# Moving two inlets of a state space layer beside its first scans, and their convolution from VectorE to TensorE

## The chip, the cores and the metric

The kernel runs on one core of a Trainium2 chip. TensorE (PE in the profile) multiplies matrices into PSUM, which the kernel uses as eight tiles filled in turn; VectorE (DVE) and ScalarE (ACT) read PSUM and work on SBUF; GpSimd (POOL) works on SBUF; SyncE (SP) and the sequencers of ACT and POOL issue DMA transfers. The metric is the device time of one execution in microseconds (us), the median over several executions.

## The reference

Two layers of a Perceiver-like block over 16 sequences of 64 tokens (1024 tokens of width 256). Layer 0 has a cross attention over 1601 context rows, a causal self attention and a feed forward part chosen by position; layer 1 has a second cross attention, a state space layer and a mixture of 64 experts. Every part adds to the residual x. The change lies in the state space layer:

```python
proj = x @ W_in.T                       # x is the layer norm of the residual
x_inner, z = proj[..., :d], proj[..., d:2 * d]          # d = 512
xc = conv(x_inner, conv_w, padding=[(3, 0)], feature_group_count=d) + conv_b
x_conv = silu(xc)                       # four taps per channel, each channel alone
dt = softplus(dt_proj + dt_bias); dA = exp(A * dt); dB = B_proj * dt
h = dA_t * h + dB_t * x_t               # scan over 64 tokens of each sequence
y_t = C_t @ h
y = (y + D * x_heads) * silu(z);  out = y @ W_out.T
```

## The kernel before, in words

The 1024 tokens are eight groups (NG = 8) of 128, two sequences in each. A group of the state space layer goes through three generators.

`inlet(g, ...)` (from L276) makes the layer norm of a group, transposes it (`psx_ss`, L285), projects it to `x_inner` (`ps_xi`, L291: eight products of 128x128x128, each of which the profile counts as two MATMULs) and to dt (`ps_dt`, L296), and copies `x_inner` to `xp`, a tile with three zeros ahead of each sequence's 64 tokens (L293). The convolution then runs channel by partition: ACT makes the first tap with the bias (L300, four instructions of 128x128) and DVE adds the other three (L304, twelve instructions of 128x128). Weights and bias are halved beforehand (`cwh`, `cbh`), so that silu is (tanh(v)+1)*v (L309, L310). Four transposes (`ps_xt`, L314) and a copy put the result in `xtok`, where the scans read it.

`sums(lo, hi)` waits for the inlets of four groups, turns their dt into softplus by a chain of small DVE instructions (L330 to L351), multiplies by a constant matrix (`ps_seg`, L356) and writes the sums to a DRAM buffer `segd` (L358, ACT's queue).

`scan(g)` computes a group's scan as matrix products over six halving levels. It loads `e` from `segd`, spread over partitions (L1336, SP's queue, two transfers of 896 KB a group), takes exponentials on ACT (L1343), projects B and C (L1350, L1357), forms `bt` (L1352), the scaled copies `pb` and `pc` (L1367 on DVE, L1369 half on POOL and half on DVE) and `pd` (L1377, POOL, reads `cT` and `bt`), projects z (L1382), forms the 128x128 matrices `gt` level by level (`ps_g`, L1400; L1408, L1417), multiplies `xtok` by them (`ps_y`, L1433), and adds the output product to x (`ps_o`, L1446, L1447). `route(g)` then picks the experts of the group and queues its rows for `post`, which scatters them with indirect DMAs on POOL (L1163).

The order in which PE gets this work is written by a planner, `drive`. Each generator yields (cost, gap): the planner advances its own clock by the cost, and calls the generator again no sooner than the gap after. Among the generators whose time has come it takes the first kind listed. The listed number is how many of one kind are open at once; a scan that has yielded "tail" no longer counts. The tile framework places instructions on each engine's queue near this order, fills the buffers of a tag in turn, and adds the waits.

There are two drives around the change. The first (L1109) holds all of layer 0 and the second cross attention, and in its list stand six inlets (g = 0 to 5, two at once) and `sums(0, 4)`. Then the pools of the first phase close, and `w2` and `wrk3` take over their memory: a tile of the second phase waits for what lay there before. The second drive (L1481) holds the inlets 6 and 7, `sums(4, 8)`, eight scans (two at once), and `outward` and `shared`. The tiles `bt`, `cT2` and `yT` of a scan have two buffers each, as `wrk3` gives by default.

Of the kernel before, what the change touches and what calls it, by code (L numbers as in the profile page):

```python
# [10 lines left out]
F32 = mybir.dt.float32  # L11
I32 = mybir.dt.int32
U32 = mybir.dt.uint32
AF = mybir.ActivationFunctionType
ALU = mybir.AluOpType
# [3 lines left out]
P = 128  # L19
B, S, D = 16, 64, 256  # L20
NTOK = B * S
NG = NTOK // P
# [8 lines left out]
DI = 512  # L31
# [110 lines left out]
def _bc(ap, axis, n):  # L142

    v = ap.unsqueeze(axis)
    shape = list(v.shape)
    shape[axis] = n
    return v.to_broadcast(shape)
# [3 lines left out]
def perceiver_kernel(ctx: ExitStack, tc: tile.TileContext, a: dict, consts: bass.AP, out: bass.AP):  # L151
    nc = tc.nc
    V, A, G, T = nc.vector, nc.scalar, nc.gpsimd, nc.tensor
# [7 lines left out]
    def const(name, rows=P):  # L161
        at, width = _COLS[name]
        return ct[:rows, at : at + width]
# [5 lines left out]
    ident = const("ident")  # L169
# [8 lines left out]
    ones = cst.tile([1, P], F32, name="ones")  # L178
# [12 lines left out]
    def evac(dst, src):  # L191

        flip[0] ^= 1
        if flip[0]:
            V.tensor_copy(dst, src)
        else:
            A.copy(dst, src)  # L197

    def layernorm(src, name, xn, parted=False, beside=None, behind=None):

        st = small.tile([P, 6], F32, tag="ln_st", name=f"st_{name}")
        V.bn_stats(st, src)
        mv = small.tile([P, 2], F32, tag="ln_mv", name=f"mv_{name}")
        V.bn_aggr(mv, st)
        ve = small.tile([P, 1], F32, tag="ln_ve", name=f"ve_{name}")
        V.tensor_scalar(ve, mv[:, 1:2], 1e-5, None, ALU.add)  # L206
        rs = small.tile([P, 1], F32, tag="ln_rs", name=f"rs_{name}")
        root = G.tensor_tensor(rs, ve, neghalf[:, 0:1], ALU.pow)  # L208
        if behind is not None:
            after(root, [behind])  # L210
        if beside is None:
            yield 0, 1.8
        else:
            for _ in range(3):
                yield next(beside)
        if parted:

            src, to = src.rearrange("p (k c) -> p k c", c=2), xn.rearrange("p (c k) -> p k c", c=2)
        else:
            to = xn  # L220
        V.tensor_scalar(to, src, mv[:, 0:1], rs, ALU.subtract, ALU.mult)
        if beside is not None:
            yield from beside
# [6 lines left out]
    pst = psm = psb  # L230
# [38 lines left out]
    sw = {"done": 0, "routed": 0, "half": 0, "made": 0}  # L269
    segd = dram.tile([NG * NH, (NL + 1) * P], F32, name="segd")  # L270

    def until(test):
        while not test():
            yield 0, 0.5

    def inlet(g, tile1, tile2):  # L276
        yield from until(lambda: "winT" in sw)
        xnT, winT = sw["xnT"], sw["winT"]
        tk = slice(g * P, (g + 1) * P)
        xn = tile1([P, D], f"xn_ss{g}")  # L280
        yield from layernorm(x[:, g, :], f"ss{g}", xn)
        yield 0, 0.9
        pt = pst([P, 2, P], f"psx_ss{g}")
        for c in range(2):
            T.transpose(pt[:, c, :], xn[:, c * P : (c + 1) * P], ident)  # L285
        evac(xnT[:, :, tk], pt)
        yield 0.3, 0.6
        pm = psm([P, 4, P], f"ps_xi_{g}")
        for j in range(4):
            for c in range(2):  # L290
                T.matmul(pm[:, j, :], lhsT=winT[:, c, j, :], rhs=xnT[:, c, tk], start=c == 0, stop=c == 1)  # L291
        xp = sw["xps"][g % 2]
        A.copy(xp[:, :, :, 3 : S + 3], pm.rearrange("p j (b t) -> p j b t", b=2))  # L293
        pm = psm([P, NH], f"ps_dt_{g}")
        for c in range(2):
            T.matmul(pm, lhsT=xnT[:, c, tk], rhs=sw["wdtT"][:, c, :], start=c == 0, stop=c == 1)  # L296
        V.tensor_tensor(sw["dtr"][:, g, :], pm, sw["dtb"], ALU.add)
        xc = tile2([P, 4, 2, S], f"xc_{g}")
        for j in range(4):
            A.activation(xc[:, j, :, :], xp[:, j, :, 0:S], AF.Identity, bias=sw["cbh"][:, j : j + 1], scale=sw["cwh"][:, j, 0:1])  # L300
        yield 2.2, 0.6
        for j in range(4):
            for k in range(1, 4):
                V.scalar_tensor_tensor(xc[:, j, :, :], xp[:, j, :, k : k + S], sw["cwh"][:, j, k : k + 1], xc[:, j, :, :], ALU.mult, ALU.add)  # L304
            if j < 3:
                yield 0, 0.8
        xcf = xc.rearrange("p j b t -> p (j b t)")
        th = tile2([P, 512], f"xth_{g}")
        A.activation(th, xcf, AF.Tanh)  # L309
        V.scalar_tensor_tensor(xcf, th, 1.0, xcf, ALU.add, ALU.mult)  # L310
        yield 0, 2.2
        pt = pst([P, 4, P], f"ps_xt_{g}")
        for j in range(4):
            T.transpose(pt[:, j, :], xcf[:, j * P : (j + 1) * P], ident)  # L314
        evac(sw["xtok"][:, g, :], pt.rearrange("p j k -> p (j k)"))
        sw["done"] += 1
        yield 0.55, 0
# [46 lines left out]
    with ExitStack() as p1:  # L364
        w1 = p1.enter_context(tc.tile_pool(name="w1", bufs=1))
        wrk = p1.enter_context(tc.tile_pool(name="wk", bufs=2))
# [7 lines left out]
        def tile1(shape, name):  # L374

            return wrk.tile(shape, F32, tag="k", bufs=15, name=name)

        def tile2(shape, name):

            return wrk.tile(shape, F32, tag="d", bufs=9, name=name)  # L380
# [46 lines left out]
        for name in ("L0_attn_q_norm_w", "L0_attn_k_norm_w"):  # L427
            src = a[name]
            nc.scalar.dma_start(
                out=rows[at[0] : at[0] + 1, :].rearrange("r (h d) -> r h d", d=HD),  # L430
                in_=_bc(src.unsqueeze(0), 1, 8),
# [86 lines left out]
        pm = psm([P, D], "ps_m0")  # L518
# [587 lines left out]
        def maker(gen, *args):  # L1106
            return lambda: gen(*args)

        drive(  # L1109
            (2, [maker(chain, 0), prepare] + [maker(chain, g) for g in range(1, NG)]),  # L1110
            (1, [prepare_ssm]),
            (2, [maker(inlet, g, tile1, tile2) for g in range(NG - 2)]),
            (1, [maker(sums, 0, 4)]),
        )

# [17 lines left out]
    xtok, xnTm = sw["xtok"], sw["xnT"]  # L1133
# [149 lines left out]
    with p2:  # L1283
        w2 = p2.enter_context(tc.tile_pool(name="w2", bufs=1, reuse_waits="tile"))
        wrk = p2.enter_context(tc.tile_pool(name="wrk3", bufs=2, reuse_waits="tile"))
# [14 lines left out]
        A.activation(Ac, col("L1_attn_A_log", 0, 4), AF.Exp)  # L1300
        V.tensor_scalar(Ac, Ac, BIG, -1.0, ALU.min, ALU.mult)


        pbs = [w2.tile([P, NL, 4, P], F32, name=f"pb{i}") for i in range(2)]
        gts = [w2.tile([P, NH, P], F32, name=f"gt{i}") for i in range(2)]
# [22 lines left out]
        def scan(g):  # L1328
# [6 lines left out]
            for q in range(2):  # L1335
                nc.sync.dma_start(  # L1336
                    out=e[q * 64 : (q + 1) * 64, :, :, :].rearrange("p j l k -> p j (l k)"),
                    in_=src[g, q].partition_broadcast(64),
# [8 lines left out]
            pm = psm([P, 4, P], f"ps_B_{g}")  # L1347
            for j in range(4):
                for c in range(2):
                    T.matmul(pm[:, j, :], lhsT=winT[:, c, 8 + j, :], rhs=xnTm[:, c, tk], start=c == 0, stop=c == 1)  # L1350
            bt = wrk.tile([P, 4, P], F32, tag="bt", name=f"bt_{g}")
            V.tensor_tensor(bt, pm, dts, ALU.mult)  # L1352
            yield 1.8, 0
            pm = psm([P, 4, P], f"ps_C_{g}")
# [4 lines left out]
            cTm = wrk.tile([P, 4, 2, P], F32, tag="cTm", bufs=1, name=f"cTm_{g}")  # L1359
            for q in range(2):  # L1360
                A.activation(cTm[:, :, q, :], pm, AF.Copy, scale=const("nsel")[:, q : q + 1])
            cT = wrk.tile([P, 4, P], F32, tag="cT2", name=f"cT_{g}")
            A.copy(cT, pm)
            pcs = []
            for l in range(NL):
# [14 lines left out]
            pm = psm([P, DI], f"ps_z_{g}")  # L1380
            for c in range(2):
                T.matmul(  # L1382
                    pm,
                    lhsT=xnTm[:, c, tk],
                    rhs=winT[:, c, 4:8, :].rearrange("p j k -> p (j k)"),
                    start=c == 0,
                    stop=c == 1,
# [7 lines left out]
            for l in range(0, NL, 2):  # L1395
                for i in range(2):
                    h = 1 << (l + i)
                    pg = psm([P, NH, 64], f"ps_g_{g}_{l + i}")
                    for j in range(4):
                        T.matmul(  # L1400
                            pg[:, 2 * j : 2 * j + 2, :].rearrange("p q t -> p (q t)"),
                            lhsT=pb[:, l + i, j, :],
                            rhs=pcs[l + i][:, j, :, :].rearrange("p q t -> p (q t)"),
                            start=True,
                            stop=True,
# [16 lines left out]
            pm = psm([P, NH], f"ps_dg_{g}")  # L1422
# [8 lines left out]
            pm = psm([P, NH, 64], f"ps_y_{g}")  # L1431
# [5 lines left out]
            pt = pst([P, 4, P], f"ps_yT_{g}")  # L1437
            for j in range(4):
                T.transpose(pt[:, j, :], yt[:, j * P : (j + 1) * P], ident)
            yT = wrk.tile([P, 4, P], F32, tag="yT", name=f"yT_{g}")  # L1440
            A.copy(yT, pt)
            yield 0.55, 0.7
            yield from until(lambda: "outward" in sw)
            pm = psm([P, D], f"ps_o_{g}")
# [30 lines left out]
        def wide(tag):  # L1475
            return lambda shape, name: wrk.tile(shape, F32, tag=tag, name=name)

        def wtile2(shape, name):
            return wide("xth" if name.startswith("xth") else "xc")(shape, name)

        drive(  # L1481
            (2, [maker(inlet, g, wide("xn"), wtile2) for g in range(NG - 2, NG)]),
            (1, [maker(sums, 4, NG)]),
            (2, [maker(scan, g) for g in range(NG)]),
            (1, [outward, shared]),
        )
# [153 lines left out]
    with tc.If(n > CAP):  # L1640
        with tc.For_i(0, E) as e:
# [9 lines left out]
            for q in range(4):  # L1651
# [12 lines left out]
                for i in range(2):  # L1664
                    g = 2 * q + i
# [36 lines left out]
```

## Time and profile before

| | |
|---|---|
| median of 7 runs | 1077.04 us (1071.03 to 1080.79) |
| profiled execution | 1066.66 us, its span 1064.9 us |
| busy share of the span | PE 80%, DVE 59%, ACT 28%, POOL 26% |
| last product of `fpy` before the first inlet | ends at 542.1 us |
| second cross attention of the last group | ends at 574.4 us |
| transposes of inlet 4, of inlets 6 and 7 | start at 588.0 and 607.4 us |
| first `e` load issued, first exponential of `e` | 606.25 and 621.66 us |
| `bt` of the eight scans | 621.4, 637.3, 670.3, 684.8, 715.0, 734.7, 765.4, 785.7 us |
| last scan adds to x | 825.2 us |
| first row of the experts gathered | 860.05 us |

A line of a group of instructions reads: line, engine, operation, output tile and input tiles, shapes, count, then the busy time in us and the mean of one in ns, then the idle time of that engine just ahead of them and what ended it. The busy time of overlapping matmuls is less than the count times the mean: sixteen MATMULs of 128 columns whose mean is 310 ns take 1.95 us together. A line of the timeline reads: start in us, duration in us, engine, line, operation and tiles, with the idle time ahead in brackets. A line of the table of stretches reads: start and end, length, then the busy time of PE, of weight loads, DVE, ACT and POOL with the number of instructions, the granted clock of TensorE as a share of full speed, the mean busy share of the DMA engines, and GB/s.

### The profile page before, as it was taken

Reading aid. Unit: us, or ns where it says so; the run is one execution under the profiler, and the core shown is the slowest. Engines: PE = TensorE matmul, PEld = TensorE weight load, DVE = VectorE, ACT = ScalarE, POOL = GpSimd, SP = SyncE. Lnnn points to the kernel's source line nnn. Section 1 sums busy time; section 2 is a strip of 40 time slices with the busy share of each in tenths; the row PEclk is TensorE's granted clock in tenths of the full one; section 3 lists DMA queues with packets and bytes.
Section 4 is the critical chain, followed back from the end, with each engine's and each line's share of the span. In section 5 each row is a group of like instructions: output and inputs, shape, how many; then the busy total and the mean of one; then the engine's idle time right before and its main releaser. Section 6 shows DMA issues by size and latency. Waiting matters only on the chain. (4 is left out here: it accounts for less than half of the span.)

```text
span 1064.9 us, 15921 instructions
## 1 busy us (share of the span) xinstructions
PE 853.1 (80%) x5858; PEld 647.5 (61%) x5858; DVE 624.7 (59%) x1863; ACT 294.8 (28%) x672; POOL 273.4 (26%) x302
## 2 busy tenths in 40 slices
PE   4978788988899788988786677978777359999956
PEld 3666555655656555555554565877666248888834
DVE  1446564466646565465566686888887863334316
ACT  0214132332332232241323353433411013323310
POOL 0000100001000101001011122455666525565650
PEclk8889999999999999999979678999887569999988
DMA  7502131310503113101501264344402958998236
GB/s 243 178 27 76 64 134 54 124 46 19 187 1 125 64 59 130 62 1 64 158 3 35 63 142 102 70 122 106 130 24 69 358 189 279 300 304 294 93 123 279
DMA packets 70725, 130.56 MB, mean 123 GB/s; under 512 B 10099, under 2 KB 56623, under 8 KB 67574
## 3 DMA queue, kind: packets, MB, share of 16 engines
q1 hardware_dynamic: 56016, 107.97, 31.3%
q0 software_dynamic: 7680, 17.33, 4.7%
q10 hardware_dynamic: 6950, 4.23, 1.4%
q8 instruction: 47, 0.77, 0.3%
q14 instruction: 32, 0.26, 0.1%
HBM read 97.54 MB, written 36.14 MB: 126 GB/s over the span
## 5 line engine op out<-in xcount | busy, mean ns | idle before, releaser
L1547 POOL DMA_INDIRECT ybuf<-yo,goal x96 | 93.5, 974 | 78.6 <-ACT yo L1573 34.2
L1539 PE MATMUL ps_ee<-xT,wq 128*128 128x192 f32 x512 | 95.4, 330 | 0.0
L1539 PEld LDWEIGHTS ps_ee<-xT,wq 128*128 128x128 f32 x512 | 81.8, 190 | 6.5 <-issue 5.8
L1163 POOL DMA_INDIRECT xbuf<-xtok,idx x64 | 69.8, 1091 | 44.2 <-issue 15.9
L994 PE MATMUL fpy<-fw,fxm 128*128 128x256 f32 x256 | 59.0, 390 | 13.3 <-DVE fxm L991 6.8
L1400 PE MATMUL ps_g<-pc,pb 128*128 128x128 f32 x384 | 56.8, 312 | 15.3 <-POOL pc L1369 7.6
L1400 PEld LDWEIGHTS ps_g<-pc,pb 128*128 128x128 f32 x384 | 55.0, 227 | 18.4 <-POOL pc L1369 16.4
L630 PE MATMUL po_a<-cn,paT_a 128*64 128x256 f32 (+1 forms) x416 | 52.8, 387 | 15.7 <-ACT paT_a L624 7.7
L994 PEld LDWEIGHTS fpy<-fw,fxm 128*128 128x128 f32 x256 | 49.3, 195 | 23.8 <-issue 15.9
L630 PE MATMUL po_b<-cn,paT_b 128*64 128x256 f32 (+1 forms) x416 | 50.2, 385 | 9.2 <-DVE paT_b L624 8.3
L208 POOL TENSOR_TENSOR rs_ff<-ve_ff,neghalf 128x1 f32<-128x1 f32 x8 | 4.4, 548 | 204.7 <-DVE ve_ff L206 193.2
L404 PE MATMUL psc<-ct,cn 128*128 128x128 f32 x384 | 50.4, 282 | 3.2 <-DVE cc_a L570 1.9
L592 PE MATMUL sc_b<-cT,qT_b 128*64 128x512 f32 (+1 forms) x256 | 47.3, 524 | 2.1 <-DVE qT_b L564 1.6
L404 PEld LDWEIGHTS psc<-ct,cn 128*128 128x128 f32 x384 | 45.3, 146 | 5.9 <-issue 3.2
L197 ACT COPY cT<-psc 128x512 f32<-128x512 f32 x51 | 29.8, 589 | 64.4 <-PE psc L404 63.9
L1541 ACT ACTIVATE hg<-ps_ee 128x192 f32<-128x192 f32 x64 | 21.2, 331 | 93.3 <-PE ps_ee L1539 93.3
L1527 PE MATMUL ps_xT<-ct,xg 128*128 128x128 f32 x192 | 30.8, 289 | 20.1 <-DMA xg<-xbuf 20.1
L592 PE MATMUL sc_a<-cT,qT_a 128*64 128x512 f32 (+1 forms) x256 | 46.4, 505 | 0.0
L630 PEld LDWEIGHTS po_a<-cn,paT_a 128*64 128x64 f32 (+1 forms) x416 | 26.8, 136 | 31.7 <-ACT paT_a L624 8.7
L630 PEld LDWEIGHTS po_b<-cn,paT_b 128*64 128x64 f32 (+1 forms) x416 | 27.7, 136 | 25.4 <-DVE paT_b L624 10.0
L208 POOL TENSOR_TENSOR rs_ml<-ve_ml,neghalf 128x1 f32<-128x1 f32 x8 | 5.6, 703 | 142.0 <-DVE ve_ml L206 142.0
L1527 PEld LDWEIGHTS ps_xT<-ct,xg 128*128 128x128 f32 x192 | 24.2, 148 | 28.5 <-DMA xg<-xbuf 20.3
(443 smaller groups left out, 1877.4 us busy)
## 6 DMA issues: line engine op xcount, KB each, us to landing
cn<-in_ctx_dram SPq DMA_DIRECT2D x16, 1536.0 KB
e<-segd SPq DMA_DIRECT2D x16, 896.0 KB
xbuf<-zero SPq DMA_DIRECT2D x8, 1632.0 KB
xg<-xbuf SPq DMA_DIRECT2D x16, 816.0 KB
wq<-in_L_ffn_We_gate_dram SPq DMA_DIRECT2D x16, 512.0 KB
wq<-in_L_ffn_We_up_dram SPq DMA_DIRECT2D x16, 512.0 KB
wq<-in_L_ffn_We_down_dram SPq DMA_DIRECT2D x16, 512.0 KB
yg<-ybuf SPq DMA_DIRECT2D x8, 1024.0 KB
```

The costliest lines, as they stand in the source:

```text
L197: A.copy(dst, src)
L208: root = G.tensor_tensor(rs, ve, neghalf[:, 0:1], ALU.pow)
L404: T.transpose(ps[:, j, :], cn[:, 4 * q + j, c * P : (c + 1) * P], ident)
L592: T.matmul(sc[b * 64 : (b + 1) * 64, :], lhsT=qT[:, c, b * 64 : (b + 1) * 64], rhs=cTs[2 * g + b][:, c, 512 * j : 512 * j + n], start=c == ...
L630: T.matmul(pos[j > 0][b * 64 : (b + 1) * 64, :], lhsT=paTs[j][:, i, b * 64 : (b + 1) * 64], rhs=cns[2 * g + b][0:r, k, :], start=k in (0, ...
L994: T.matmul(py, lhsT=xm[:, t, c, :], rhs=fw[:, 2 * h + t, c, :], start=h + t + c == 0, stop=h == 3 and t == 1 and c == 1,)
L1163: sct = G.indirect_dma_start(out=xbuf, out_offset=bass.IndirectOffsetOnAxis(ap=idx[:, g, k : k + 1], axis=0), in_=xtok[:, g, 0:DX], in_off ...
L1400: T.matmul(pg[:, 2 * j : 2 * j + 2, :].rearrange("p q t -> p (q t)"), lhsT=pb[:, l + i, j, :], rhs=pcs[l + i][:, j, :, :].rearrange("p q t ...
L1527: T.transpose(to, xgs[q][:, 2 * part + s, c * P : (c + 1) * P], ident)
L1539: T.matmul(pe[:, j, :], lhsT=w, rhs=xTs[q][:, i, c, :], start=c == 0, stop=c == 1)
L1541: A.activation(hg, pe[:, 0, :], AF.Silu)
L1547: arr = G.indirect_dma_start(out=ybuf, out_offset=bass.IndirectOffsetOnAxis(ap=goal, axis=0), in_=y, in_offset=None, bounds_check=NTOK * T ...
```

## The change

Inlets 4 and 5 leave the first drive and stand with 6 and 7 in the second, again two at once, beside the scans. In the second phase an inlet finds `taps`, sixteen diagonal 128x128 matrices (four channel blocks, four taps) made there by DVE, and `cbr`, the halved bias as a row, which comes by a DMA on ACT's queue and a multiplication on POOL. Its convolution is then sixteen products of a diagonal with a shifted view of `xp`, and four products of the bias row with a row of ones, all accumulated in one PSUM tile `ps_cv`; tanh and the last product read that tile, and ACT alone copies the transposed result. Inlets 0 to 3 keep their convolution on ACT and DVE. `bt`, `cT2` and `yT` get one buffer each.

```diff
@@ inlet
         V.tensor_tensor(sw["dtr"][:, g, :], pm, sw["dtb"], ALU.add)
+        if "taps" in sw:
+            yield 2.2, 1.0
+            pm = psm([P, 4, P], f"ps_cv_{g}")
+            for j in range(4):
+                for k in range(4):
+                    T.matmul(pm[:, j, :].rearrange("p (b t) -> p b t", b=2), lhsT=sw["taps"][:, j, k, :], rhs=xp[:, j, :, k : k + S], start=k == 0, stop=False)
+                T.matmul(pm[:, j, :], lhsT=sw["cbr"][:, j * P : (j + 1) * P], rhs=ones, start=False, stop=True)
+            th = tile2([P, 512], f"xth_{g}")
+            pmf = pm.rearrange("p j k -> p (j k)")
+            A.activation(th, pmf, AF.Tanh)
+            xcf = tile2([P, 512], f"xc_{g}")
+            V.scalar_tensor_tensor(xcf, th, 1.0, pmf, ALU.add, ALU.mult)
+            yield 4.2, 2.0
+            pt = pst([P, 4, P], f"ps_xt_{g}")
+            for j in range(4):
+                T.transpose(pt[:, j, :], xcf[:, j * P : (j + 1) * P], ident)
+            A.copy(sw["xtok"][:, g, :], pt.rearrange("p j k -> p (j k)"))
+            sw["done"] += 1
+            yield 0.55, 0
+            return
         xc = tile2([P, 4, 2, S], f"xc_{g}")
@@ first drive
-            (2, [maker(inlet, g, tile1, tile2) for g in range(NG - 2)]),
+            (2, [maker(inlet, g, tile1, tile2) for g in range(NG // 2)]),
@@ second phase
+        taps = sw["taps"] = w2.tile([P, 4, 4, P], F32, name="taps")
+        for j in range(4):
+            V.tensor_tensor(taps[:, j, :, :], _bc(ident, 1, 4), _bc(sw["cwh"][:, j, :], 2, P), ALU.mult)
+        cbr = sw["cbr"] = w2.tile([1, DI], F32, name="cbr")
+        nc.scalar.dma_start(out=cbr, in_=a["L1_attn_conv_b"].unsqueeze(0))
+        G.tensor_scalar(cbr, cbr, 0.5, None, ALU.mult)
@@ scan: bufs=1 for three tags
-            bt = wrk.tile([P, 4, P], F32, tag="bt", name=f"bt_{g}")
+            bt = wrk.tile([P, 4, P], F32, tag="bt", bufs=1, name=f"bt_{g}")
-            cT = wrk.tile([P, 4, P], F32, tag="cT2", name=f"cT_{g}")
+            cT = wrk.tile([P, 4, P], F32, tag="cT2", bufs=1, name=f"cT_{g}")
-            yT = wrk.tile([P, 4, P], F32, tag="yT", name=f"yT_{g}")
+            yT = wrk.tile([P, 4, P], F32, tag="yT", bufs=1, name=f"yT_{g}")
@@ second drive
-            (2, [maker(inlet, g, wide("xn"), wtile2) for g in range(NG - 2, NG)]),
+            (2, [maker(inlet, g, wide("xn"), wtile2) for g in range(NG // 2, NG)]),
```

## The prediction

> **What bounds the kernel now.** I read the page's slices first: the middle of the span is where PE drops below 8 tenths and its granted clock sinks.
>
> ```profile
> PE   4978788988899788988786677978777359999956
> DVE  1446564466646565465566686888887863334316
> PEclk8889999999999999999979678999887569999988
> ```
>
> The seam between inlets and scans is slices 22 to 25 (559 to 665 us; a slice is 26.6). To see what it consists of I cut it into stretches, from the transposes of inlet 4 (587.8) to the end of scan 2's B product (670.3), the point to which I compare, and the next two pairs of scans.
>
> ```profile
> 587.80:597.70 9.90, 7.05 (x47) 6.35 (x47) 7.52 (x27) 4.76 (x11) 4.51 (x3) 0.81 0.01 2
> 597.70:608.50 10.80, 5.86 (x16) 2.50 (x16) 7.72 (x25) 3.35 (x8) 0.00 (x0) 0.53 0.30 80
> 608.50:620.20 11.70, 11.66 (x77) 10.35 (x76) 7.00 (x28) 6.12 (x14) 0.00 (x0) 0.85 0.98 210
> 620.20:626.90 6.70, 0.03 (x1) 0.06 (x1) 5.42 (x9) 5.00 (x9) 3.01 (x3) 0.65 0.75 152
> 626.90:643.70 16.80, 15.78 (x92) 14.34 (x92) 16.23 (x37) 6.52 (x12) 4.37 (x4) 0.73 0.48 110
> 643.70:649.60 5.90, 0.02 (x1) 0.05 (x2) 5.70 (x8) 0.87 (x3) 4.10 (x3) 0.71 0.00 0
> 649.60:670.30 20.70, 19.81 (x140) 16.55 (x141) 10.07 (x20) 9.57 (x17) 2.63 (x3) 0.92 0.42 96
> 670.30:715.00 44.70, 36.48 (x259) 32.92 (x257) 40.00 (x129) 18.27 (x37) 23.66 (x21) 0.96 0.44 108
> 715.00:765.40 50.40, 39.97 (x275) 36.16 (x273) 42.64 (x131) 14.98 (x33) 30.92 (x29) 0.90 0.47 118
> ```
>
> In the first seven, 82.5 us, PE is busy 60.2 and idle 22.3; where it idles DVE is nearly full, and the clock is 0.53 to 0.85. PE's own waits there:
>
> ```profile
> PE ps_seg L356 <- DVE sp_dt L351: 7.8, 2, 5.9
> PE ps_g L1400 <- DVE pb L1367: 6.7, 1, 6.7
> PE ps_xt L314 <- DVE xc L310: 3.7, 2, 1.9
> PE psx_ss L285 <- DVE xn_ss L221: 1.2, 1, 1.2
> ```
>
> So the seam is paced by DVE (convolutions, softplus chain, pb and pc), and the first `e` load stands behind inlet 5's convolution, as SP's waits say:
>
> ```profile
> SPq L1336 <- DVE xc L310: 27.5, 1, 27.5
> SPq L1336 <- PE ps_xt L314: 1.2, 1, 1.2
> ```
>
> **The prices.**
>
> ```profile
> 573.75 1.95 PE L291 MATMUL ps_xi<-xnTm,winT 128*128 128x128 f32 x16
> 649.58 3.17 PE L356 MATMUL ps_seg<-kmat,sp_dt 128*32 128x512 f32 x4 [5.94 <-DVE sp_dt L351]
> L304 DVE SCALAR_TENSOR_TENSOR xc<-xp,cwh,xc 128x128 f32<-128x128 f32 x96 | 27.5, 351 | 0.8 <-ACT xc L300 0.6
> L1590 DVE TENSOR_TENSOR dgl<-ct,w 128x512 f32<-128x512 f32 x8 | 5.5, 689 | 0.2
> ```
>
> *Convolution on PE.* At full clock 16 MATMULs take 1.95 us, 0.122 each. One inlet has 16 diagonal products and 4 bias products, two MATMULs each: 40 x 0.122 = 4.9 us. Four inlets: 19.5 us added to PE. The bias products have one row of weights; the nearest row with few rows (`ps_ohb`, 8 rows, at a poor clock) is 3.6 us for 16, 0.225 each, so the 32 bias MATMULs cost 3.9 to 7.2; I take 3.9, as the shape streamed is the same 128 columns.
>
> [...]
>
> *Taken from DVE and ACT.* 48 of the L304 instructions lie in the 82.5 us (13.5 us of DVE, the group's total in that stretch) and 16 of L300 (6.6 of ACT). All go. Added to DVE: `taps`, four 128x512 products like L1590, 2.8 us. They run after the softplus chain and before the first convolution, while PE does the projections of inlets 4 and 5 (2 x 2.5 with dt); cost nothing, and up to 2.8 if that cover is gone. Three evacuations of `ps_xt` leave DVE (0.69 each), ACT takes them at 0.59.
>
> *The rest of the build.* `cbr`'s DMA is one more issue on ACT's queue (0.35 like Db's) and POOL's multiplication waits for it, with two `pb` memsets (2.66 each) and the rsqrt of a layer norm (0.55) queued behind. Those memsets are needed only by the first pb, some 20 us later; nothing on the path, 0 to 2.
>
> *Layer norms of inlets 4 and 5.* No new instruction; their rsqrt moves past the memsets on POOL. In before the later inlets' statistics run as early as 575.4, so 0.
>
> *The first `e` load.* The chain of sums(0, 4) breaks off at 591.03 and waits for inlet 4's dt, then shares DVE with L304, and ends at 597.55. Without them its last seven links of 0.21 end at 592.5; `ps_seg` to the write's issue takes 3.7 in the second sums (649.58 to 653.28), so 596.2 instead of 600.78; the write's traffic ends 2 us after issue. The load then issues near 598.4, 7.8 us before 606.25.
>
> *Order on PE.* From the yields: xi4, xi5, conv4, conv5, xt4, B0, xt5, C0, z0, xi6, g0 (first two levels), conv6, xi7, xt6, g0, conv7, g0, xt7, dg0, B1, y0, C1, z1, seg, g1... In before, the planner's order and PE's timeline agree step for step. So all 19.5 us stand ahead of scan 2: the second convolution pair is planned between scan 0's levels.
>
> **The sum.** Of the 60.2 us that PE is busy, instructions at their rate with a full clock make 54.0 (xi 7.8, dt 2.0, transposes 4.8, B, C and z 13.6, levels 11.7, y 3.8, seg 5.1, dg 1.9, o 2.0, the rest 1.3), and the low clock 6.2. After: 54.0 + 19.5 = 73.5, plus what stays:
> - low clock in the first 20 us: xi4 +1.2, the next xi +1.7 (3.69 against 2.0), transposes +0.9: 3.8 (bounds 1 to 6.2);
> - PE waits for the chain of sums(0, 4): as now, 2.9 (0 to 3.9);
> - transposes and evacuations at the start: 2.2 (1.2 + 0.5 + 0.5; 1 to 3);
> - first levels waiting for `pb` (6.7 now): C0 is followed by z0, xi6 and a transpose, 5 us of cover, and the exponentials have their data 7.8 us sooner; 1 (0 to 6.7);
> - seg of sums(4, 8) waiting for DVE (5.9 now): DVE falls from 59.7 to some 47 us in the stretch; 1.5 (0 to 5.9);
> - pc and yT waits as now, 1.7.
>
> That is 73.5 + 13.1 = 86.6 against 82.5: **+4.1 us**. From there scans 2 and 3 come in the order that scans 4 and 5 have now; the planner makes that pair 1.1 longer, the rows 44.7 and 50.4 bound it at 0 and 5.7; I take 1.1, since the longer pair also carries more POOL work (30.9 against 23.7). Sum **+5 us**. The profiled execution, 1066.7 us with 1.8 around its span, becomes 1072; the runs' median stands 10.4 above it: **1082**.
>
> The row for the clock is the table: 0.53 after PE idled, 0.92 when it was dense. [...]
>
> *Single buffers.* bt of scan g+1 must now wait for pd of scan g on POOL. Ends of pd and starts of the next bt: 680.85 and 684.83, 730.69 and 734.67, 781.29 and 785.70; the least margin is 4.0 us. `cT2` and `yT` have more. Cost 0, but behind a bt on DVE stand pb, pc and the routing.
>
> **Rivals.**
> 1. *The scans are paced by `e`, not by PE, and all move up with it.* For it: 7.8 us earlier, and PE's 22.3 us idle could hold 19.5. Against: the cold and starting terms remain. Price -7.8: 1069; the low bounds below give -5.3 in the seam, and the rest would come out of the 8.2 us that PE idles in the next pair. The sign turns when what stays idle or cold is under 9.0 us (82.5 - 73.5) instead of 13.1.
> 2. *The waits of the first scans stay.* The pb and seg waits at 6.7 and 5.9 instead of 2.5: +10.1 more, 1092. For it: B1 now comes after conv7, and bt1, pb1, pc1 and the softplus chain fall together on DVE. Against: DVE is 13 us lighter.
> 3. *The single buffers bind.* Four posts at 1.28 us ahead of a pd delay it by 5.1, 1.1 past the margin, three times: +3.4, 1085; each bt after an even scan.
>
> **How the numbers follow.** About 0.5% (5.4 us) is what a measurement can tell from no change. The forecast has 0.47 (0.15 within that, 0.32 above; its own range 1077 to 1089), rival 1 0.25 (0.21 faster, 0.04 same), rival 2 0.19 and rival 3 0.09, both slower. Faster 0.21, same 0.19, slower 0.60. All terms at their low bounds give 73.5 + 3.7 = 77.2, -5.3; at their high ones 73.5 + 27.4 + 2.8 + 3.3 + 2.0 + 5.7, +32. The range cuts that to rival 1 less 1 and rival 2 plus 4: 1068 to 1096.
>
> **What would show it.** Right: `e` issued near 598; no L304 past 586; 160 MATMULs of `ps_cv` at 0.12 each; PE over 90% busy from 605 to 665 with a clock near 1.0; bt of scan 1 near 647 instead of 637, of scan 2 at 670 to 676; later pairs about 50 us. Wrong: idle PE ahead of the first `ps_g` or seg as long as now, DVE's bt waiting for pd, or ps_cv dearer than 4.9 us an inlet.

## The result, and the profile after

The changed kernel takes 1082.8 us, the median of 28 runs, against 1076.45 us for 70 runs of the kernel before: a ratio of 1.0057, 95% interval 1.0044 to 1.0070. It is slower by 6.1 us (0.57% of 1076.45); forecast were 1082 us and +5.

The profiled execution has a span of 1074.6 us, 9.7 more than before's 1064.9. Part of that has nothing to do with the change: the projection of inlet 2, ahead of everything that the edit touches, starts at 576.30 us instead of 573.75, and in the fourteen profiled executions of this study that start lies anywhere between 573.75 and 587.95. So below, times of two kernels are compared from the start of inlet 2's projection, and changes of time are taken from the medians and ratios of all runs. Counted so, the last scan adds to x 257.9 us after that start, and 251.4 before: +6.5. That is near the medians' +6.1, but it is one execution of each kernel, and the part behind scan 2's `bt` scatters by several us, as the table of the experiments will show.

The page's slices (40 equal parts of the span, busy tenths, and the granted clock of TensorE):

```profile
PE   4888788988899788988786699878977349999956
DVE  1446565466646565466655456787978773343316
PEclk8789999999999999999988799988987569999988
```

Where PE fell to 6 and 7 tenths before, it now has one slack place at the start of the seam and is then full, and DVE has sunk in the seam. The stretches begin at the same point as the prediction's, moved by the offset of 2.55 us between the two starts (587.80 becomes 590.35; the transposes of inlet 4, which began there before, now come at 603.3). The first seven end with the product y of scan 1, which before lay ahead of scan 2's B and now lies behind it; the last two are the next two pairs of scans (start and end, length, busy time of PE, weight loads, DVE, ACT and POOL, clock, share of DMA, GB/s):

```profile
590.35:600.20 9.85, 0.57 (x4) 0.17 (x2) 9.01 (x27) 0.00 (x0) 5.95 (x4) 0.50 0.16 51
600.20:609.00 8.80, 8.77 (x49) 5.77 (x49) 1.26 (x4) 2.21 (x5) 0.00 (x0) 0.77 0.23 55
609.00:621.40 12.40, 12.40 (x85) 10.48 (x86) 0.85 (x2) 1.32 (x3) 0.00 (x0) 1.00 0.99 207
621.40:634.00 12.60, 10.44 (x82) 9.14 (x81) 7.53 (x9) 9.26 (x15) 5.00 (x4) 1.00 0.30 60
634.00:650.30 16.30, 16.30 (x122) 14.40 (x120) 11.77 (x34) 4.58 (x8) 1.22 (x1) 1.00 0.53 114
650.30:661.30 11.00, 11.00 (x85) 9.62 (x84) 5.85 (x14) 7.43 (x15) 1.78 (x2) 1.00 0.01 2
661.30:678.30 17.00, 15.88 (x119) 13.62 (x119) 11.83 (x19) 5.49 (x14) 7.21 (x6) 1.00 0.52 116
678.30:726.40 48.10, 37.70 (x253) 34.18 (x252) 42.40 (x128) 16.26 (x34) 25.13 (x21) 0.89 0.40 100
726.40:774.30 47.90, 41.27 (x275) 37.18 (x274) 41.80 (x132) 17.24 (x35) 30.67 (x28) 0.89 0.51 124
```

The seam is 87.95 us long (the first seven lines) against 82.5: +5.45. In it PE is busy 75.4 us instead of 60.2 and idle 12.6 instead of 22.3. From 600.2 to 661.3 it is busy 58.9 of 61.1 us. The next pairs are 48.1 and 47.9 against 44.7 and 50.4, together +0.9. The idle time that is left lies in three places, as PE's waits in the seam show (the second is inlet 6's projection, at 629.7):

```profile
PE ps_seg L377 <- DVE sp_dt L372: 9.3, 1, 9.3
PE ps_xi L291 <- ACT xnTm L197: 2.2, 1, 2.2
PE ps_o L1474 <- DVE woT L195: 0.9, 1, 0.9
```

The waits of 6.7 us for pb and 5.9 us for the second sums are gone; the one for the first sums, 1.9 us before, is 9.3. So nine microseconds of idle time sit where the projections of inlets 4 and 5 were. The timeline on that place shows why the sums are late:

```profile
591.03 2.66 POOL L1335 MEMSET pb<- 128x3072 f32 x1 [9.86 <-DMA Db<-in_L_attn_D_dram]
591.56 2.16 DVE L364 TENSOR_SCALAR sp_po<-sp_r 128x32 f32<-128x32 f32 x1
591.64 2.08 DVE L1326 TENSOR_TENSOR taps<-ct,cwh 128x512 f32<-128x512 f32 x1
```

The same link in the kernel before:

```profile
588.87 0.17 DVE L343 TENSOR_SCALAR sp_po<-sp_r 128x32 f32<-128x32 f32 x1
```

This link of the chain, 0.17 us before, takes 2.16 (L364) and ends at 593.72, where POOL's memset ends (593.69); the diagonals queue between the links.

And the price of the products, the timeline of PE in the first block of 128 channels of inlet 4 and the start of the next:

```profile
608.96 1.14 PE L304 MATMUL ps_cv<-xp,taps 128*128 128x128 f32 x8
610.03 0.48 PE L305 MATMUL ps_cv<-ones,cbr 1*128 1x128 f32 x2
610.44 1.16 PE L304 MATMUL ps_cv<-xp,taps 128*128 128x128 f32 x8
```

A block starts every 1.50 us, so an inlet costs 6.0 us of a dense PE (one that never waits) at full clock (granted 1.00 from 609.0 to 621.4 and from 634.0 to 650.3), and the four 24.0.

### The profile page after: what moved, and what is told of

The parts are those of the page before. It is cut to its first block, busy times and chain, and to the rows that moved or that the text cites. A ratio compares the mean times of both kernels' runs of the same rounds, so it can differ in the third digit from the quotient of the medians.

```text
span 1074.6 us, 16181 instructions
## 1 busy us (share of the span) xinstructions
PE 872.9 (81%) x6018; PEld 664.6 (62%) x6018; DVE 614.0 (57%) x1817; ACT 289.2 (27%) x658; POOL 278.0 (26%) x303
## 5 line engine op out<-in xcount | busy, mean ns | idle before, releaser
L1575 POOL DMA_INDIRECT ybuf<-yo,goal x96 | 93.4, 973 | 79.5 <-ACT yo L1601 32.6
L1184 POOL DMA_INDIRECT xbuf<-xtok,idx x64 | 71.0, 1110 | 47.6 <-DVE dg L1454 20.9
L425 PE MATMUL psc<-ct,cn 128*128 128x128 f32 x384 | 50.6, 283 | 3.4 <-DVE cc_a L591 2.1
L1397 POOL TENSOR_TENSOR pc<-cTm,e 128x512 f32<-128x512 f32 x24 | 35.3, 1505 | 43.9 <-ACT cTm L1389 43.8
```

The source lines that it names most:

```text
L425: T.transpose(ps[:, j, :], cn[:, 4 * q + j, c * P : (c + 1) * P], ident)
L1184: sct = G.indirect_dma_start(out=xbuf, out_offset=bass.IndirectOffsetOnAxis(ap=idx[:, g, k : k + 1], axis=0), in_=xtok[:, g, 0:DX], in_off ...
L1397: (V if l % 2 else G).tensor_tensor(pc.rearrange("p j q (k h) -> p j q k h", h=1 << l), cTm.rearrange("p j q (k u h) -> p j q k u h", u=2, ...
L1575: arr = G.indirect_dma_start(out=ybuf, out_offset=bass.IndirectOffsetOnAxis(ap=goal, axis=0), in_=y, in_offset=None, bounds_check=NTOK * T ...
```

## The experiments

Theory T, formed from this: behind the first sums PE runs dense, so its time is the price (24.0 us of products), and the wait of 9.3 us at the start is the rest. Rival A: it is the place, inlets 4 and 5 beside the scans, whatever convolves them. Rival B: the single buffers. Rival C: the `e` loads and DVE pace the seam, and PE has room. Later theory M: the memsets on POOL hold the first sums.

All landmarks in one table, from each kernel's timeline, in us after the start of inlet 2's projection: the first `ps_seg`, B of scan 0, `bt` of scan 2, the lengths from there to `bt` of scan 4 and on to that of scan 6, and the last addition to x. In the changed kernel and those with its order (no bias products, one bias product, taps on ACT, memsets later, bias on ACT) y of scan 1, 2 us of PE, comes behind `bt` 2, in the others ahead of it. Ratios are to the kernel before, run beside each on the same chip, with 95% intervals; 0.25% is 2.7 us. The difference of two ratios has an interval of its own, about 0.25 to 0.3% to either side.

The landmarks are from one execution of each kernel. Three kernels have before's order and times within 0.24% of each other: before, single buffers, and memsets later in the kernel before. They agree within 1.0 us at `bt` of scan 2 (96.6 to 97.6), but not behind it: their last x is at 251.4, 257.2 and 257.1. So the columns up to `bt` 2 can be compared to about a microsecond, and the last three can't, where before's order is one side of the comparison.

| kernel | median, us | ratio | ps_seg | B0 | bt 2 | 2 to 4 | 4 to 6 | last x |
|---|---|---|---|---|---|---|---|---|
| before | 1076.45 | | 23.95 | 40.9 | 96.6 | 44.7 | 50.4 | 251.4 |
| changed | 1082.80 | 1.0057 [1.0044, 1.0070] | 23.89 | 45.2 | 99.8 | 50.3 | 47.9 | 257.9 |
| single buffers | 1080.41 | 1.0024 [0.9996, 1.0053] | 24.22 | 41.2 | 96.8 | 45.4 | 55.4 | 257.2 |
| place alone | 1083.58 | 1.0058 [1.0033, 1.0084] | 21.94 | 31.5 | 99.5 | 47.6 | 49.4 | 256.7 |
| products for two | 1104.90 | 1.0259 [1.0219, 1.0299] | 25.98 | 70.4 | 114.9 | 50.6 | 56.7 | 282.0 |
| no bias products | 1075.42 | 0.9983 [0.9959, 1.0007] | 24.32 | 40.7 | 93.4 | 50.1 | 47.8 | 251.3 |
| one bias product | 1079.27 | 1.0013 [0.9992, 1.0034] | 24.21 | 43.0 | 97.0 | 50.0 | 47.8 | 254.6 |
| taps on ACT | 1084.04 | 1.0059 [1.0033, 1.0086] | 22.97 | 44.7 | 99.4 | 50.7 | 48.0 | 257.5 |
| front halves | 1081.88 | 1.0033 [1.0005, 1.0061] | 26.35 | 47.7 | 99.8 | 45.4 | 50.1 | 254.9 |
| three mends | 1087.38 | 1.0106 [1.0071, 1.0141] | 26.69 | 53.2 | 105.8 | 45.4 | 50.5 | 261.4 |
| memsets later | 1082.58 | 1.0055 [1.0028, 1.0081] | 22.27 | 44.2 | 98.9 | 50.8 | 48.0 | 257.1 |
| memsets later, before | 1079.26 | 1.0009 [0.9978, 1.0040] | 22.22 | 39.9 | 97.6 | 46.0 | 53.6 | 257.1 |
| bias on ACT | 1079.47 | 1.0013 [0.9990, 1.0037] | 21.49 | 37.7 | 93.7 | 50.0 | 47.7 | 251.4 |
| all mends | 1078.11 | 1.0005 [0.9977, 1.0034] | 23.46 | 39.3 | 95.7 | 45.7 | 50.3 | 252.7 |

**Single buffers: the kernel before with one buffer for three tags.**

```diff
-            bt = wrk.tile([P, 4, P], F32, tag="bt", name=f"bt_{g}")
+            bt = wrk.tile([P, 4, P], F32, tag="bt", bufs=1, name=f"bt_{g}")
...                                # cT2 and yT alike
```

> The kernel before with bt, cT2 and yT in one buffer instead of two; nothing else changed. Theory T (the loss is TensorE's own time for the convolutions plus a start that waits for sums(0, 4); the single buffers cost nothing): within 2 us of before, no bt waits for a pd on POOL. Rival B (the single buffers bind, half or more of the loss is theirs): slower by 3 us or more, and bt in the later pairs waits for pd. In the trace of the changed kernel bt never waited for pd, so I expect T.

Measured +0.24%, 2.6 us, with an interval from -0.4 to +5.7 us: between the two expectations, and it decides nothing by itself. In its trace the seam is as before (bt 2 at 96.8), no `bt` waits for a `pd`, and the 5 us come in the pair 4 to 6. The kernel before with its memsets held back, which has two buffers, shows 53.6 in the same pair and a time within 0.1%. So it seems that the pair scatters in before's order, by 3 to 5 us between profiled executions; two profiles of one kernel, which would show it, are not there. I found no wait that the buffers make; that they cost a microsecond or two stays possible.

**Place alone: the changed kernel without the diagonals, all inlets convolving on ACT and DVE.**

```diff
-        taps = sw["taps"] = w2.tile([P, 4, 4, P], F32, name="taps")
...
-        G.tensor_scalar(cbr, cbr, 0.5, None, ALU.mult)
```

> The changed kernel without the diagonals and the bias row: inlets 4 to 7 stand beside the scans, but convolve on ACT and DVE as in the kernel before. Theory T: the place costs little in itself, since PE has 20 to 24 us less to do than in the changed kernel; but DVE carries the convolutions of four inlets (4 x 6.8 us = 27 us, of which 13.5 were there before), so the time is between 3 us below and 3 us above before. Rival A (moving inlets 4 and 5 beside the scans costs, whatever engine convolves): slower than before by 5 us or more, as much as the changed kernel or more. If DVE, and not TensorE, paces this seam, then also slower by up to 13 us: this is told from A by the stretch from the transposes of inlet 4 to B of scan 2: under A PE waits in it for the e loads, otherwise for xc and sp_dt on DVE.

Measured +0.58%, as much as the changed kernel, outside what T allowed (within 3 us of before). The stretch was to tell which of the other two it is. From the point that corresponds to 587.80 (594.85 here) to scan 2's `bt` it is 85.6 us long, against 82.5 before; PE is busy 61.0 of it and DVE 60.4, against 60.2 and 59.7. PE's longest waits there all end on DVE:

```profile
PE ps_g L1420 <- DVE pb L1387: 7.8, 1, 7.8
PE ps_xt L335 <- DVE sp_up L356: 6.2, 2, 4.1
PE ps_seg L377 <- DVE sp_dt L372: 4.8, 1, 4.8
```

PE itself waits for no `e` load, but ahead of the longest of these waits DVE does, through the exponentials on ACT:

```profile
620.49 3.41 ACT L1363 ACTIVATE e<-e,Ac 128x768 f32<-128x768 f32 x4 [1.03 <-DMA e<-segd]
623.99 2.97 DVE L1387 TENSOR_TENSOR pb<-bt,e 128x256 f32<-128x256 f32 x2 [2.77 <-ACT e L1363]
```

So most of PE's idle time waits for work on DVE (the convolutions and the chains), and some 2.8 us of it for `e`: both readings have a part. The move with the old convolution costs about 6 us, as much as the changed kernel. This kernel has the single buffers too, so that their 0.24%, if it is real, is in the 0.58%. With the products PE no longer waits for DVE but is full itself; the kernel takes the same time. T was wrong to count the place at nothing.

**Products for two: only inlets 6 and 7 beside the scans, with products.**

```diff
-            (2, [maker(inlet, g, wide("xn"), wtile2) for g in range(NG // 2, NG)]),
+            (2, [maker(inlet, g, wide("xn"), wtile2) for g in range(NG - 2, NG)]),
...                                # and six inlets in the first drive
```

> The changed kernel with only inlets 6 and 7 beside the scans, as before, and their convolutions as products; inlets 4 and 5 back in the first stage with ACT and DVE. Theory T: half of the products, 12 us of TensorE instead of 24; the chain of sums(0, 4) no longer stands behind the taps but is as before (the first write of segd within 1 us of before's): before + 1 to + 4 us, that is 2 to 5 us below the changed kernel. Rival A (the place is what costs): equal to before, within 1.5 us, since the place is undone. Rival C (TensorE has room, the seam is paced by the e loads and DVE): below before by 2 us or more, since DVE loses 13.5 us of convolutions.

Measured +2.6%, 28 us, which no theory had. The trace shows what happened up to scan 2, 18.3 us of it: PE's queue has the projections and convolutions of both inlets ahead of scan 0's B, which starts at 70.4 instead of 40.9, although the exponentials of `e` are there by 51; the bias row arrives late (2.7 us of waiting); and then PE runs at half clock, as its timeline shows:

```profile
628.83 0.48 PE L305 MATMUL ps_cv<-ones,cbr 1*128 1x128 f32 x2 [2.71 <-POOL cbr L1329]
...
631.20 2.08 PE L304 MATMUL ps_cv<-xp,taps 128*128 128x128 f32 x8
633.21 0.79 PE L305 MATMUL ps_cv<-ones,cbr 1*128 1x128 f32 x2
```

From 631.0 to 648.5 PE is busy all 17.5 us with a granted clock of 0.50, and a block takes 2.72 us instead of 1.50. The other 12 us lie in the two pairs that follow (50.6 and 56.7); up to 5 of them are within the scatter of these pairs, and the rest I haven't traced to a cause. As a test of half the products this run is void: it changed the order of PE's queue as well.

**No bias products: the four bias products of an inlet left out, and with them the bias of groups 4 to 7.**

```diff
-                T.matmul(pm[:, j, :], lhsT=sw["cbr"][:, j * P : (j + 1) * P], rhs=ones, start=False, stop=True)
```

> The changed kernel without the four bias products of each inlet: the convolution of inlets 4 to 7 is left without its bias, and so is the output. Theory T (after the first stage's end TensorE runs dense, its time is the price): the 16 bias products take 8.2 us of TensorE (2.04 us an inlet), and 6 to 8.5 us go: 1074 to 1077 against 1082.8 for the changed kernel, about level with before. Rival C (the seam is paced by the e loads and the chain on DVE): under 2 us go.

The ratio falls by 0.74%, 8.0 us (about 5 to 11 with the interval), and `bt` of scan 2 comes 6.4 us earlier, with the later pairs unchanged (50.1 and 47.8). That is T's number and speaks against C: in this order, a microsecond taken from PE's products is most of a microsecond of the kernel. It also gives the price of each part:

```profile
612.24 7.39 PE L304 MATMUL ps_cv<-xp,taps 128*128 128x128 f32 x64
619.47 0.60 PE L313 MATMUL ps_xt<-ct,xc 128*128 128x128 f32 x4
```

From start to start 64 MATMULs take 7.23 us, 0.113 each: 3.6 us an inlet for the diagonals, 14.5 for four. The rest of the 24.0, 9.5 us, are the 32 MATMULs of the bias, 0.30 each.

**One bias product: four rows by 512 columns instead of four products of one row.**

```diff
+            T.matmul(pm.rearrange("p j k -> p (j k)"), lhsT=sw["cbr"], rhs=sw["rows4"], start=True, stop=False)
...
-                T.matmul(pm[:, j, :], lhsT=sw["cbr"][:, j * P : (j + 1) * P], rhs=ones, start=False, stop=True)
```

> The changed kernel with the bias of an inlet as one product of 4 rows with 512 columns (weights 4 x 128, the four blocks of the bias; the moved matrix has ones in the block of each row) instead of four products of one row with 128 columns. In the changed kernel the four take 2.04 us an inlet; one product of 512 columns takes 0.9 to 1.0 us (ps_z, four such products, 1.88 for 2 x 2 MATMULs). Theory T (from the end of sums(0, 4) TensorE's time is the price): 1.1 us an inlet, 4.4 us in all, so 3.5 to 5 us below the changed kernel, about 1078. Rival C (the seam is paced by DVE and the e loads): under 1.5 us below it.

The ratio falls by 0.44%, 4.7 us with an interval from 2 to 7; at the last x it is 3.3 us. That is T's size (3.5 to 5) and more than C allowed (under 1.5). PE's timeline gives 1.05 us for the bias and 3.77 for the diagonals, 4.8 an inlet instead of 6.0, so 4.7 us in four:

```profile
621.00 1.12 PE L302 MATMUL ps_cv<-rows,cbr 4*128 4x512 f32 x2
622.05 3.84 PE L305 MATMUL ps_cv<-xp,taps 128*128 128x128 f32 x32
```

**Taps on ACT: the diagonals built by sixteen activations.**

```diff
-            V.tensor_tensor(taps[:, j, :, :], _bc(ident, 1, 4), _bc(sw["cwh"][:, j, :], 2, P), ALU.mult)
+            for k in range(4):
+                A.activation(taps[:, j, k, :], ident, AF.Copy, scale=sw["cwh"][:, j, k : k + 1])
```

> The changed kernel with its diagonals built by 16 activations on ACT instead of four products on DVE. In the changed kernel DVE spends 4.6 us on the diagonals within the chain of sums(0, 4), which ends no earlier than in the kernel before, while TensorE waits 9.3 us for it. Theory T (the diagonals stand on the path that ends the start): the chain ends some 4 us earlier, ps_seg and the e loads with it, the wait of 9.3 us falls to about 5, and the time falls by 2 to 5 us below the changed kernel. Rival: other work on DVE or the memsets that slow it fill the place, and under 1 us goes.

Nothing is gained: `ps_seg` comes only 0.9 us earlier and the time is the same. The rival was right: the first link still takes 2.16 us beside the memset of pb, and a layer norm queued there 2.21.

**Front halves: layer norm, transposes and projections of inlets 4 and 5 back in the first drive, the products where they are.**

```diff
-            (2, [maker(inlet, g, tile1, tile2) for g in range(NG // 2)]),
+            (2, [maker(inlet, g, tile1, tile2) for g in range(NG // 2)] + [maker(inlet, g, tile1, tile2, "front") for g in (4, 5)]),
```

> The changed kernel with the first halves of inlets 4 and 5 (layer norm, transposes, the projections to xi and dt) in the first stage, where the kernel before has them; their convolutions as products stay beside the scans. Theory T (the wait of 9.3 us at the start is a hole that moved with inlets 4 and 5): TensorE does the two projections (4.9 us) while it waits for sums(0, 4), the hole falls to 3 to 5 us, and 4 to 6 us go: about 1077. Rival A (it is the place of the convolution that costs): the time stays within 1.5 us of the changed kernel. A third way, seen in the kernel with products for two inlets, is that the order on TensorE puts B of scan 0 later; here it stands behind the convolutions of inlets 4 and 5 and the projection of inlet 6, so that B of scan 0 should start no later than in the changed kernel.

The ratio falls by 0.24%, 2.6 us: between the two expectations, and within the noise of the comparison, so that only the trace speaks. PE's wait for the first sums falls from 9.3 to 4.0 us, as T said, but the sums themselves now wait for the two inlets' dt on DVE and end 2.5 us later (26.35), and B of scan 0 comes at 47.7, later than the expectation had it. With y of scan 1 counted in both, the seam is 99.8 against 102.0: of the 5.3 us by which the wait shrank, 2.2 came through.

**Three mends: the last three together.**

> The changed kernel with all three: one bias product an inlet, diagonals built on ACT, and the first halves of inlets 4 and 5 in the first stage. Theory T: the three gains lie in different places (4.4 us of TensorE's time, 2 to 5 us of the chain, of which the earlier projections take the same hole in part), so 7 to 12 us below the changed kernel: 1070 to 1076, at or below before. If the seam is paced by DVE and the e loads instead: 1079 to 1083.

Slower than any of them, +1.06%. The matrix with ones for the bias product is copied on ACT behind the sixteen activations for the diagonals, and PE waits for it ahead of the first convolution:

```profile
PE ps_cv L306 <- ACT rows L1336: 5.2, 1, 5.2
```

B of scan 0 is 8 us later than in the changed kernel, and 5.5 later than with the front halves alone. The gains did not add, for the most part because two of them put their work on one queue.

**Memsets later: the four memsets of pb and gt wait for the last link of the first sums; in the changed kernel, and in the kernel before.**

```diff
-            G.memset(t, 0.0)
+            after(G.memset(t, 0.0), [sw["dt0"]])    # the chain's last instruction
```

> The changed kernel with the four memsets of pb and gt on POOL held back until the last link of sums(0, 4) on DVE is done; they do the same work. In the traces DVE's links of 0.17 to 0.19 us take 2.16 us when a memset runs on POOL beside them, in the changed kernel and with the diagonals built on ACT alike, so that the chain ends at the same place in both. Theory M (the memsets, not the diagonals, hold the chain): 16 links of 0.22, four diagonals that add some 0.47 each and two layer norms of 0.4 give 6.2 us from the first polynomial link (15.3 us after the projection of inlet 2) to the last, so ps_seg comes 2 to 3 us earlier, TensorE's wait falls from 9.3 to 6 or 7, and 1.5 to 3 us go, to 1079.5 to 1081. Rival: something else holds the chain, ps_seg comes at the same place and nothing goes.

> The kernel before with the same four memsets held back until the last link of sums(0, 4). In it a memset stretches one link of the chain to 2.22 us, so the chain can end up to 2 us earlier; but inlet 5's convolution on DVE and the e loads behind it stand where they did. Theory M with DVE pacing the kernel before: 0 to 2 us below before. If the memsets, held back, run beside the convolutions of inlets 4 and 5 instead, DVE's work there is stretched by up to 7 us: slower by 1 to 4.

M's mechanism holds, its worth does not. The same link beside the same diagonal, without a memset:

```profile
601.38 0.17 DVE L364 TENSOR_SCALAR sp_po<-sp_r 128x32 f32<-128x32 f32 x1
601.46 0.68 DVE L1326 TENSOR_TENSOR taps<-ct,cwh 128x512 f32<-128x512 f32 x1
```

0.17 and 0.68 us instead of 2.16 and 2.08. The chain ends 1.6 us earlier instead of 2 to 3, PE's wait is 7.2 us, and the time is the same within the interval (1.0055 against 1.0057); in the trace 0.8 us are gained at the last x. What stays of the wait is the length of the chain itself, with nothing on PE to fill it: from this link to the last it is 8.6 us long in the changed kernel, 6.5 here, and 4.1 in the kernel of the place alone, which has neither memsets nor diagonals among the links. The kernel before doesn't change either (+0.09%).

**Bias on ACT, and all mends: memsets later, the bias added by ACT ahead of the tanh; then the front halves as well.**

```diff
+            for j in range(4):
+                A.activation(xcf[:, j * P : (j + 1) * P], pm[:, j, :], AF.Identity, bias=sw["cbh"][:, j : j + 1])
+            A.activation(th, xcf, AF.Tanh)
+            V.scalar_tensor_tensor(xcf, th, 1.0, xcf, ALU.add, ALU.mult)
...
-                T.matmul(pm[:, j, :], lhsT=sw["cbr"][:, j * P : (j + 1) * P], rhs=ones, start=False, stop=True)
```

> The changed kernel with the memsets held back as in the run beside it, and with the bias added on ACT (four activations of 128 columns ahead of the tanh, 1.65 us an inlet as the kernel before's first tap takes) instead of by products: TensorE has 8.2 us less to do, the result is the full one. Theory T: level with the kernel that left the bias out (1075.4 against 1077.3 before in its own comparison), less the 1.5 to 3 us of the memsets, plus up to 1 us for ACT's step: 0.2 to 0.5% below before. If the seam is paced by ACT and DVE once TensorE is relieved: level with before or above.

> The kernel of the run beside it (memsets held back, bias on ACT), with the first halves of inlets 4 and 5 in the first stage as well. By the run that moved the halves alone, 2.6 us less than without; theory T: 0.3 to 0.7% below before. If the wait at the start, once the memsets are gone, no longer covers the two projections, the gain is under 1 us.

Both are quicker than the changed kernel, by 0.44% and 0.52% of before's time (4.7 and 5.6 us), and level with the kernel before: +0.13% and +0.05%, with intervals that hold 1. Expected were 0.2 to 0.7% below it. Bias on ACT gives back what the bias products cost up to scan 2 (93.7 against 99.8) and keeps the longer pair 2 to 4; with the front halves y of scan 1 moves back into the seam, which is then 2 us longer, and the pair 4 shorter. In the trace PE then waits 8.6 us for the products' way through ACT and DVE (`ps_xt` for xc), and the halves' gain alone of 2.6 us isn't found again (0.08% between the two ratios). No version beat the kernel before by what can be measured.

## Why the prediction was right, and where it was not

**The time and the sign.** Forecast +5 and 1082; measured +6.1 and 1082.8. In plain words: the products need 24.0 us of PE, the seam had 22.3 us of idle PE, 9.3 us of the idle time came back as a wait at the start, and from there on PE is full and everything else waits for it. The mechanism was right in its main part: PE takes on the products, becomes full, and the waits of pb and of the second sums go. By the prediction's own stretches: seam +4.1, measured +5.45; pairs +1.1, measured +0.9, which the scatter of these pairs doesn't let one tell from 0 or from several us less. That the sum came so near is in good part luck: three of its terms were too low, by 13 us together, and three too high, by 12:

| term, us | predicted | measured | |
|---|---|---|---|
| convolution on PE | 19.5 | 24.0 | start of a block every 1.50 |
| all other work of PE, with the low clock | 54.0 + 3.8 | 51.4 | 75.4 busy less 24.0 |
| wait for the first sums | 2.9 | 9.3 | first line of the waits |
| transposes and evacuations at the start | 2.2 | 0 | no wait there |
| inlet 6's projection waiting for its transposes | 0 | 2.2 | second line |
| pb, second sums, pc and yT | 1 + 1.5 + 1.7 | 1.1 | ps_o for woT, 0.9 and 0.2 |
| seam | 86.6 | 87.95 | |

- *Convolution on PE.* The diagonals were right, 14.5 against 15.6. The bias was the mis-sized term: 9.5 us against 3.9, and above the upper bound of 7.2. The step that failed is "I take 3.9, as the shape streamed is the same 128 columns": the row with few weights, `ps_ohb` (0.225), was the near one, and the truth (0.30) lay beyond it. The shifted views of `xp` show no price of their own: the diagonals take 0.113 us a MATMUL, the sixteen of inlet 2's projection 0.112 from their start to the next group's (576.30 to 578.09 in the changed kernel).
- *All other work of PE.* The 54.0 adds up the busy times of groups, and groups that follow each other overlap at their ends: in the changed kernel's seam the groups other than the products add up to 58.3 us, of which 51.4 are left once the overlaps count once. Taken from 60.2 us of busy time, in which overlaps count once, such a sum leaves too little for the low clock. What came back in the denser seam is 60.2 - 51.4 = 8.8 us, where I had 2.4 (6.2 - 3.8); the mean granted clock of the seam rose from 0.77 to 0.92, and groups of the same count became shorter (`ps_xi` 10.9 to 8.2 us, `ps_g` 13.9 to 11.7, B 7.1 to 5.9).
- *The first `e` load*, predicted 7.8 us earlier through a chain that ends at 592.5. Reduced by the offset of 2.55, the chain ends at 597.6 as it did before, the load issues at 603.4 instead of 606.25, and the wait for the first sums is 9.3, outside its bounds (0 to 3.9; the "as now, 2.9" was itself 1.0 too much, the line says 7.8 less 5.9). The step was "its last seven links of 0.21 end at 592.5" together with the diagonals, which were to "run after the softplus chain", and the memsets as "nothing on the path": the chain now runs on without the wait for inlet 4's dt, but diagonals and memsets stand between its links. By the lengths of the chain in three kernels (8.6, 6.5 and 4.1 us) the memsets cost it some 2.1 us and the diagonals 2.4.
- *The waits of pb and the second sums* went, as predicted (2.5 left was too cautious); rival 2 is refuted by the waits above. *DVE* fell to 48.1 us in the seam, predicted some 47.
- *Single buffers*, cost 0: no `bt` waits for a `pd` in either trace; the comparison alone leaves 0 to 6 us open.
- *Rival 1*, a gain of 7.8, had its turning point at 9.0 us idle or cold; 12.6 us of idle time alone were left. The run without bias products, 0.9983, shows that it was the nearest other case: with the bias free, the kernel would have been level.
- *What would show it.* `bt` of scan 2 at 673.6 by the offset lay in the forecast 670 to 676, the pairs near 50, PE busy 96% from 600 to 661 at a clock of 0.77 up to 609 and 1.00 from there; `bt` of scan 1 came at 653.0 instead of 647. Of the signs of error two were there, the dearer `ps_cv` and the idle PE ahead of the first `ps_seg`.

What the prediction did not see at all is that the place costs as much with the old convolution (1.0058, single buffers included). I took the move as free and the products as the price; the runs show a seam in which PE either waits, mostly for DVE, or is full with the products, and the six microseconds are lost either way.

## What to carry to other kernels

Moving work from an engine that paces a stage to one that idles there pays only while the receiver's idle time exceeds the work at its true price; here 22.3 us of idle PE met 24.0 us of products, and a wait of 1.9 us at the start grew to 9.3 because the work that had filled it was moved away too. Price a product with few rows of weights by a measured one, and ask whether the bias can ride on an instruction of another engine that is there anyway. When an experiment moves a generator to another place, compare the order of the queue first: one that changes it tests the order, not the part.

## What the runs showed of the hardware

- In the changed kernel a DVE instruction beside a POOL memset lasted until the memset ended: 2.16 us for a link of 0.17, which ended 0.03 us after the memset (593.72 against 593.69), and 0.17 when the memset came later. Not all did: beside the next memsets (595.11 to 596.97) a TENSOR_SCALAR of 128x4 (`Ac`) took 0.77 us, against 0.26 with the memsets later, and ended 0.04 us after them, while a TENSOR_TENSOR link took its 0.19. No run shows what decides it. The kernel before had it too: its link at 593.50 took 2.22 us, where others of its line took 0.18, and ended 0.03 us after the memset of 2.66 us that began at 593.03. The prediction, which costed the memsets at nothing with a bound of 2, should have weighed it.
- In the changed kernel a product with one row of weights and 128 columns cost more than one with 128 rows: 0.30 us a MATMUL among the diagonals, 0.113 for theirs. The 0.30 is a difference (a block's 1.50 us less eight times 0.113, halved) and includes whatever the change between the two kinds costs; no run has one-row products by themselves. One with 4 rows and 512 columns took 1.05 us for two MATMULs (one bias product).
- The clock stayed at 0.50 for 17.5 us in which PE was busy without a gap (products for two), while the same products ran at 1.00 in the changed kernel. In the run for two it had been 0.93 just before, from 625 to 631, a stretch that holds the wait of 2.71 us for the bias row, and it was 0.91 again in the 12.2 us that begin with B of scan 0. In the changed kernel PE had no such wait among the products: its waits in the seam, of 9.3, 2.2, 0.9 and 0.2 us, are for other tiles. What kept the clock low was not tested.
- The start of the same code, ahead of everything changed, lay between 573.75 and 587.95 us in fourteen profiled executions: 14.2 us, more than the 6.1 of this change.
